# A mixture of experts on one core: the second product of five experts by seven block products, and the searches for their tokens in two queues

## The chip, the cores and the metric

The kernel runs on one core of one Trainium2 chip. The metric is the device time of one execution in microseconds (us). Before the change it is 1454.23 us, the median of 3 runs (1453.94 to 1454.76). The engines are called as in the profile: PE (TensorE: matmuls, and PEld for its weight loads), DVE (VectorE), ACT (ScalarE), POOL (GpSimd, which also issues the indirect DMAs) and SP (SyncE, which issues DMAs).

## What is computed

Four sublayers follow each other on 4 x 1024 tokens of 256 numbers, each with a layer norm and a residual. The first three are an attention in groups, a low-rank feed-forward and a 16-head attention with relu weights; the change does not touch them. The fourth is a mixture of 8 experts in which each expert chooses its own 1024 of the 4096 tokens:

```python
def _L1_ffn_ref(x, Wg, W1, b1, W2, b2):
    n = b * l                                   # 4096 tokens
    k = min(max(int(n * C / e), 1), n)          # 1024 for each of 8 experts
    xt = x.reshape(n, h)                        # h = 256
    S = jax.nn.sigmoid(xt @ Wg).T
    G, I = jax.lax.top_k(S, k)
    ex = xt[I]
    hid = jax.nn.gelu(jnp.einsum('ekh,ehf->ekf', ex, W1) + b1[:, None, :], approximate=False)
    out = (jnp.einsum('ekf,efh->ekh', hid, W2) + b2[:, None, :]) * G[..., None]   # 1024 -> 256
    new_x = jnp.zeros_like(xt).at[I.reshape(-1)].add(out.reshape(-1, h))
```

All matmuls spoken of here are in f32.

## The kernel before

The expert part begins at about 960 us of the span. Tokens are held in 32 tiles of 128 (NTILE), an expert's 1024 chosen tokens in 8 chunks of 128 (NC = 8). An expert is worked in two halves of 512 tokens (TB = 512, NJ = 4 chunks each); `u = 2 * e + q` counts the halves through all experts.

**Search and list.** The top 1024 scores of an expert are found by a search for the threshold, bit by bit. `Search` does it for several experts at once: `compare` (lines 1819 to 1831) compares the scores with seven tried values, one VectorE instruction (L1824) per expert, and counts (L1831); a `tick` (L1833) adds the counts up over the partitions by one small matmul (L1838), keeps the best value on VectorE and compares again. `List` turns a threshold into indices: `sort`, `rank`, `chunks`, `places` (VectorE, L1971), `collect` (matmuls, L1981) and `gather`, which makes the indices and starts eight indirect DMAs on GpSimd (L2005) that fetch the token rows `got`. The search and list of expert 0 stand ahead of the expert part. All others are steps of one list, `agenda`: Search(1), the list of 1, Search(2, 3), the lists of 2 and 3, Search(4, 5, 6, 7), the lists of 4 to 7. Each step carries an estimate of its VectorE time and the first half `u` in which it may be done (`behind`). `go_on_with_lists(u, time)` (L2357) is called at many places of the matmul loops with the time that has passed there, and hands out the next step when the last one is reckoned to be done. Three pieces of Search(1), a compare and two ticks, are written ahead of the first half (loop at L2380).

**First product.** `turn` (L2168) transposes the gathered rows by TensorE (L2176) and copies them to `xT` (L2182). In `feed_forward` (L2276) a half has eight steps `f`, each with two matmuls of 512 columns (L2291) and a gelu on ScalarE into `hid` (L2298). Experts 3 to 6 take both halves together in `feed_forward_by_seven` (L2226): the 2 x 2 block product (blocks over the 256 inputs, the 1024 hidden numbers and the two halves) is made with seven block products of sums and differences instead of eight. It has four steps `f`, each with seven matmuls (L2237), five additions on VectorE (L2252 to L2266) and four gelus. The sums of weight blocks that it needs are made by four GpSimd instructions (`weight_sums`, L2201), the sums of token blocks by four VectorE instructions (`token_sums`, L2208).

**Second product.** `project_back` (L2308) goes over the four chunks of a half: eight matmuls of 256 columns into one PSUM tile (L2317), `y = (py + bias) * gate` in two VectorE instructions (L2332, L2333), and an indirect DMA on GpSimd that adds the rows `y` to their tokens in DRAM (L2334). An expert's scatters wait for the ones of the expert before. There are seven `y` tiles. The transposes of the next half stand between the chunks (`turns_within`, L2210). Expert 7 adds to `accg` instead (L2328), and works on the closing layer norm beside its matmuls (`aside`).

The order on each engine is that in which the program writes the instructions, save where the tile scheduler moves one; for GpSimd it is the written order from expert 6 on (`manual_schedule`). Rooms that the change uses again: `accg` and `xg`, two 128 x 8 x 256 tiles that expert 7 needs at the end, and `wq1`, `wk1`, `wv`, weights of the third sublayer.

Of the kernel before, what the change touches and what calls it, by code (L numbers as in the profile page):

```python
# [9 lines left out]
F32 = mybir.dt.float32  # L10
# [3 lines left out]
AF = mybir.ActivationFunctionType  # L14
ALU = mybir.AluOpType
# [4 lines left out]
P = 128  # L20
D = 256
DC = D // P
TB = 512
# [51 lines left out]
def kernel(  # L75
# [1679 lines left out]
    with ExitStack() as st4:  # L1755
# [135 lines left out]
        class List:  # L1891
# [58 lines left out]

            def steps(self):

                behind = max(QPE * self.e - 3, 0)
                return [
                    (0.5, behind, self.sort),
                    (2.6, behind, self.rank),
                    (1.2, behind, self.chunks),
                    (1.4, behind, lambda: (self.places(0), self.places(1))),
                    (1.4, behind, lambda: (self.places(2), self.places(3))),
                    (0.3, behind, lambda: [self.collect(part) for part in range(4)]),  # L1960

                    (0.3, behind + 1, self.gather),
                ]

            def places(self, part):
# [199 lines left out]
        QPE = NC // NJ  # L2165
        xT = {}

        def turn(u, c, half=None):  # L2168

            if c == 0 and not half:  # L2170
                xT[u] = wk.tile([P, DC, TB], F32, tag="xT", name="xT")
            e, q = divmod(u, QPE)
            tiles = range(NJ) if half is None else range(half * NJ // 2, (half + 1) * NJ // 2)
            tp = ps.tile([P, NJ, P], F32, tag="mm", name="tp", bufs=5)
            for i in tiles:
                nc.tensor.transpose(tp[:, i, :], lists[e].got[q * NJ + i][:, c * P : (c + 1) * P], ident)  # L2176
                if u == 0 and c == 0 and i == 0:

                    keep_busy(first, 4)
            cols = slice(tiles[0] * P, (tiles[-1] + 1) * P)  # L2180
            copy = nc.scalar.copy if by_seven(e) else nc.vector.tensor_copy
            copy(xT[u][:, c, cols], tp.rearrange("p j t -> p (j t)")[:, cols])  # L2182

        def by_seven(e):

            return 3 <= e < NE - 1

        rooms = [x.rearrange("p j d -> p (j d)")[:, h * TB : (h + 1) * TB] for x in xs[:4] for h in range(2)]
        seven = dict(zip(("sum0", "T1", "sum1", "T2", "T4", "S1", "S2", "S4"), rooms))
# [13 lines left out]
        def token_sums(e, n):  # L2203

            (b11, b21), (b12, b22) = ([xT[QPE * e + q][:, c, :] for c in range(DC)] for q in range(QPE))
            t1, t2, t4 = (seven[name] for name in ("T1", "T2", "T4"))
            dst, x, y = ((t1, b12, b11), (t2, b22, t1), (b12, b22, b12), (t4, b21, t2))[n]
            nc.vector.tensor_tensor(dst, x, y, ALU.subtract)  # L2208

        def turns_within(u):  # L2210

            e, q = divmod(u, QPE)
            if u == QPE * NE - 1:
                return {}
            turns = {c: (lambda c=c: turn(u + 1, c)) for c in range(DC)}
            if q == QPE - 1 and by_seven(e + 1):
                both = [
                    turns[0], turns[1], lambda: turn(u + 2, 0), lambda: token_sums(e + 1, 0), lambda: turn(u + 2, 1),
                    *(lambda n=n: token_sums(e + 1, n) for n in (1, 2, 3)),
                ]  # L2220
                return {0: both[0:1], 1: both[1:4], 2: both[4:]}
            if by_seven(e) and q == 0:
                return {}
            return {2: [turns[0], turns[1]]} if u == 1 else {1: [turns[0]], 2: [turns[1]]}

        def feed_forward_by_seven(e):  # L2226

            w1, w2 = weights[e]
            hid = [wk.tile([P, FC, TB], F32, tag="hid", name="hid") for _ in range(QPE)]
            (b11, b21), (t3, b22) = ([xT[QPE * e + q][:, c, :] for c in range(DC)] for q in range(QPE))  # L2230
            t1, t2, t4 = (seven[name] for name in ("T1", "T2", "T4"))
            half = DFF // 2
            s3 = w1[:, 0, half:DFF]
            s1, s2, s4 = (seven[name] for name in ("S1", "S2", "S4"))

            def product(bank, a, b, start, stop, f):
                nc.tensor.matmul(bank, lhsT=a[:, f * P : (f + 1) * P], rhs=b, start=start, stop=stop, skip_group_check=not start)  # L2237

            gelus = []

            def gelu(n, f, src):
                gelus.append(nc.scalar.activation(hid[n][:, f, :], src, AF.Gelu, bias=mb1[:, e * FC + f : e * FC + f + 1]))

            HC = FC // 2
            for f in range(HC):
                a, b, c, d = (ps.tile([P, TB], F32, tag="mm", name=f"ph{k}", bufs=5) for k in range(4))
                u2 = seven[f"sum{f % 2}"]
                c22, c21, c12 = hid[1][:, HC + f, :], hid[0][:, HC + f, :], hid[1][:, f, :]
                product(a, w1[:, 0, 0:half], b11, True, True, f)
                nc.scalar.copy(u2, a)  # L2250
                product(b, s2, t2, True, True, f)
                nc.vector.tensor_tensor(u2, u2, b, ALU.add)  # L2252
                product(c, s3, t3, True, True, f)
                nc.vector.tensor_tensor(c22, u2, c, ALU.add)
                product(d, s1, t1, True, True, f)
                nc.vector.tensor_tensor(c22, c22, d, ALU.add)
                product(a, w1[:, 1, 0:half], b21, False, True, f)
                gelu(0, f, a)
                if f < HC - 1:
                    go_on_with_lists(QPE * e, 3.2, True)  # L2260
                gelu(1, HC + f, c22)
                product(c, w1[:, 1, half:DFF], t4, False, True, f)
                nc.vector.tensor_tensor(c21, u2, c, ALU.add)
                gelu(0, HC + f, c21)
                product(d, s4, b22, False, True, f)
                nc.vector.tensor_tensor(c12, u2, d, ALU.add)  # L2266
                gelu(1, f, c12)
                go_on_with_lists(QPE * e, 3.0)
            for q in range(QPE):
                if q == 0 and by_seven(e + 1):  # L2270
                    weight_sums(e + 1, gelus[-1])
                if q == 0 and e == NE - 2:
                    fetch_last()
                project_back(QPE * e + q, hid[q])

        def feed_forward(u):  # L2276
            e, q = divmod(u, QPE)
            w1, w2 = weights[e]
            hid = wk.tile([P, FC, TB], F32, tag="hid", name="hid")

            n = TB if u else TB // 2
            for h in range(TB // n):
# [3 lines left out]
                for f in range(FC):  # L2286
# [13 lines left out]
                    )  # L2300
                    if u or h or f not in (FC - 5, FC - 4, FC - 3):
                        go_on_with_lists(u, 1.75 if u else 0.87)
                    aside(u, "f", f)
            if q == QPE - 1 and by_seven(e + 1):
                weight_sums(e + 1, gelu)
            project_back(u, hid)

        def project_back(u, hid):  # L2308

# [2 lines left out]
            ahead = turns_within(u)  # L2312
            for i in range(NJ):
                k = q * NJ + i
                py = ps.tile([P, D], F32, tag="y", name="py")
                for f in range(FC):
                    nc.tensor.matmul(  # L2317
                        py,
                        lhsT=hid[:, f, i * P : (i + 1) * P],
                        rhs=w2[:, f, :],  # L2320
                        start=(f == 0),
                        stop=(f == FC - 1),
                    )
                for do in ahead.get(i, ()):
                    do()
                gates = lists[e].got[k][:, D + e : D + e + 1]
                if e == NE - 1:
                    nc.vector.scalar_tensor_tensor(accg[:, k, :], py, gates, accg[:, k, :], ALU.mult, ALU.add)  # L2328
                    aside(u, "i", i)
                    continue  # L2330
                y = wk.tile([P, D], F32, tag="y", name="y", bufs=7)
                nc.vector.tensor_tensor(y, py, mb2[:, e, :], ALU.add)  # L2332
                nc.vector.tensor_scalar(y, y, gates, None, ALU.mult)  # L2333
                scatter = nc.gpsimd.indirect_dma_start(  # L2334
# [7 lines left out]
                )  # L2342
                after_all(scatter, scattered[e - 1] if e else ())
                beside_each_other(scatter, scattered[e])
                go_on_with_lists(u, 3.4 if by_seven(e) else 2.3)

        searches = [Search(0), Search(1), Search(2, 3), Search(4, 5, 6, 7)]
        agenda = []  # L2350
        for search in searches[1:]:
            agenda.extend(search.steps())
            for e in search.es:
                agenda.extend(lists[e].steps())
        left = [0.0]

        def go_on_with_lists(u, time, within=False):  # L2357
            left[0] = max(left[0] - time, 0.0)
            if agenda and left[0] < 0.3 and agenda[0][1] <= u and not (within and agenda[0][0] not in (0.5, 1.2, 1.4)):
                spent, _, step = agenda.pop(0)  # L2360
                left[0] += spent
                step()

        first = ps.tile([P, TB], F32, tag="mm", name="idle", bufs=5)
        def first_places():
# [12 lines left out]
            if step == lists[0].rank:  # L2378
                keep_busy(first, 8)
        for _ in range(3):  # L2380
            agenda.pop(0)[2]()
            keep_busy(first, 4)
        def fetch_last():

# [49 lines left out]
```

## Time and profile before

| | |
|---|---|
| median of 3 runs | 1454.23 us |
| profiled execution: its time, its span | 1461.5 us, 1459.7 us |
| mean granted TensorE clock of it | 0.983 |
| busy in the span: PE, DVE, ACT, POOL | 1407.1, 863.5, 735.9, 531.2 us |
| second product, L2317: 1024 records of matmuls | 230.6 us busy, mean 382 ns |
| first product, L2291: 288 records | 114.8 us busy |
| scatters, L2334: 56 | 88.1 us busy on POOL |
| window 1050 to 1110 us: PE, DVE, ACT, POOL busy | 60.00, 29.35, 11.26, 21.20 us |
| window 1110 to 1170 us | 59.64, 41.52, 13.50, 25.41 us |
| window 1333 to 1388 us, granted clock 0.97 | 51.87, 24.34, 13.15, 27.27 us |
| window 1388 to 1460 us, granted clock 0.95 | 61.90, 39.56, 26.90, 40.78 us |

A row of the groups view reads: line, engine, operation, output <- inputs, shape, count, then busy time in us, mean duration of one in ns, then the idle time before the instructions with what ended it. Matmuls overlap in the array, so the mean duration of one is longer than the distance from one to the next; the distance is read from the timeline, where a row gives start, length and the number of records in it. An f32 matmul leaves two records.

### The profile page before, as it was taken

Reading aid. Unit: us, or ns where it says so; the run is one execution under the profiler, and the core shown is the slowest. Engines: PE = TensorE matmul, PEld = TensorE weight load, DVE = VectorE, ACT = ScalarE, POOL = GpSimd, SP = SyncE. Lnnn points to the kernel's source line nnn. Section 1 sums busy time; section 2 is a strip of 40 time slices with the busy share of each in tenths; the row PEclk is TensorE's granted clock in tenths of the full one; section 3 lists DMA queues with packets and bytes.
Section 4 is the critical chain, followed back from the end, with each engine's and each line's share of the span. In section 5 each row is a group of like instructions: output and inputs, shape, how many; then the busy total and the mean of one; then the engine's idle time right before and its main releaser. Section 6 shows DMA issues by size and latency. Waiting matters only on the chain.

```text
span 1459.7 us, 26465 instructions
## 1 busy us (share of the span) xinstructions
PE 1407.1 (96%) x10392; PEld 859.7 (59%) x10392; DVE 863.5 (59%) x2133; ACT 735.9 (50%) x1014; POOL 531.2 (36%) x662
## 2 busy tenths in 40 slices
PE   8999999999889999999999999949999999999997
PEld 4666666666644445454454547717666656756674
DVE  5457555666454637664757486885545766355246
ACT  4244454444368887878778788712221232232143
POOL 4123322322352223423333223413425325543655
PEclk9999999999999999999999999979999999999998
DMA  8400000001652373537244711152414223333365
GB/s 223 140 1 1 0 1 1 1 1 40 206 166 83 115 223 94 154 117 233 73 142 149 227 59 35 46 163 41 106 26 121 50 84 69 78 97 58 76 168 133
DMA packets 104853, 138.76 MB, mean 95 GB/s; under 512 B 25469, under 2 KB 64794, under 8 KB 104602
## 3 DMA queue, kind: packets, MB, share of 16 engines
q1 hardware_dynamic: 74512, 81.75, 18.2%
q0 software_dynamic: 30160, 55.32, 16.3%
q8 instruction: 81, 1.33, 0.4%
q14 instruction: 42, 0.34, 0.1%
q10 hardware_dynamic: 58, 0.01, 0.0%
HBM read 75.29 MB, written 61.51 MB: 94 GB/s over the span
## 4 chain that ended last, share of the span: by engine, by line
PE 86%; DVE 6%; issue 2%; DMA 2%; POOL 2%; ACT 1%; another core or an unknown queue 1%; SPq 0%; POOLq 0%; DVEq 0%; ACTq 0%
PE po L1553 16%; PE py L2317 14%; PE sc L1532 10%; PE ph L2237 7%; PE ph L2291 7%; PE pg L722 4%; PE pv L738 4%; PE py L848 3%; PE pt L1308 2%; PE pq L397 2%; PE po L820 2%; PE ph L904 2%; PE pv L431 2%; PE po L824 1%; PE pkv L835 1%
## 5 line engine op out<-in xcount | busy, mean ns | idle before, releaser
L1710 ACT ACTIVATE w<-sc 128x1024 f32<-128x1024 f32 x395 | 379.9, 1023 | 60.8 <-PE sc L1532 60.2
L1553 PE MATMUL po<-w,vaug 128*17 128x256 f32 (+1 forms) x4608 | 256.0, 358 | 1.5 <-DVE turned L1611 1.2
L2317 PE MATMUL py<-w,hid 128*128 128x256 f32 x1024 | 230.6, 382 | 3.1 <-DVE y L2332 3.1
L2317 PEld LDWEIGHTS py<-w,hid 128*128 128x128 f32 x1024 | 193.1, 191 | 33.5 <-issue 4.4
L1712 DVE TENSOR_SCALAR w<-sc 128x1024 f32<-128x1024 f32 x117 | 142.4, 1220 | 79.5 <-PE sc L1532 76.1
L1553 PEld LDWEIGHTS po<-w,vaug 128*17 128x17 f32 x4608 | 116.3, 97 | 118.0 <-issue 48.3
L1532 PE MATMUL sc<-q,kT 64*128 64x512 f32 (+1 forms) x1152 | 170.3, 404 | 2.5 <-ACT w L1710 1.3
L1532 PEld LDWEIGHTS sc<-q,kT 64*128 64x128 f32 x1152 | 89.9, 185 | 83.5 <-issue 46.7
L2334 POOL DMA_INDIRECT acc_d<-y,idx x56 | 88.1, 1574 | 119.8 <-DVE y L2333 59.5
L2298 ACT ACTIVATE hid<-ph,mb 128x512 f32<-128x512 f32 (+1 forms) x72 | 46.1, 640 | 164.8 <-PE ph L2291 137.2
L2291 PE MATMUL ph<-xT,w 128*128 128x512 f32 (+1 forms) x288 | 114.8, 552 | 0.3 <-DVE xT L2182 0.3
L2005 POOL DMA_INDIRECT got<-tok_d,idx x64 | 66.9, 1045 | 113.0 <-DVE idx L1995 96.0
L2291 PEld LDWEIGHTS ph<-xT,w 128*128 128x128 f32 x288 | 52.6, 190 | 51.3 <-issue 48.5
L371 POOL DMA_DIRECT2D kT<-k_d x32 | 23.4, 732 | 118.4 <-PE sc L1532 55.4
L2332 DVE TENSOR_TENSOR y<-py,mb 128x256 f32<-128x256 f32 x56 | 23.5, 420 | 71.8 <-PE py L2317 51.7
L722 PE MATMUL pg<-nT,wh 128*128 128x512 f32 x128 | 61.6, 613 | 1.5 <-ACT nT L661 1.5
L848 PE MATMUL py<-wo,oT 128*128 128x256 f32 x256 | 61.6, 384 | 0.0
L738 PE MATMUL pv<-wh,nT 128*128 128x512 f32 x128 | 59.7, 592 | 0.0
L848 PEld LDWEIGHTS py<-wo,oT 128*128 128x128 f32 x256 | 47.5, 190 | 17.6 <-issue 11.1
L746 ACT ACTIVATE v<-v 128x512 f32<-128x512 f32 x32 | 20.2, 630 | 62.7 <-DVE v L745 62.7
L1137 POOL TENSOR_TENSOR rsb<-veb,mhalf 128x1 f32<-128x1 f32 x30 | 19.6, 653 | 86.8 <-DVE veb L1136 86.8
L586 POOL TENSOR_TENSOR x<-x,y 128x1024 f32<-128x1024 f32 x13 | 30.6, 2355 | 56.3 <-ACT y L575 56.3
(352 smaller groups left out, 2338.0 us busy)
## 6 DMA issues: line engine op xcount, KB each, us to landing
q<-q_d POOLq DMA_DIRECT2D x16, 1024.0 KB
kT<-k_d POOLq DMA_DIRECT2D x32, 512.0 KB
w<-in_L_ffn_W_dram SPq DMA_DIRECT2D x16, 1024.0 KB
k_d<-parts SPq DMA_DIRECT2D x48, 256.0 KB
q_d<-parts SPq DMA_DIRECT2D x48, 256.0 KB
acc_d<-logits SPq DMA_DIRECT2D x8, 512.0 KB
tok_d<-hg SPq DMA_DIRECT2D x30, 128.0 KB
x<-in_L_attn_x_dram SPq DMA_DIRECT2D x7, 512.0 KB
```

The lines of the kernel that those rows point to most:

```text
L722: nc.tensor.matmul(pg, lhsT=wh[:, c, HID + e * P : HID + (e + 1) * P], rhs=d["nT"][:, c, :], start=(c == 0), stop=(c == DC - 1),)
L738: nc.tensor.matmul(pv, lhsT=d["nT"][:, c, i * P : (i + 1) * P], rhs=wh[:, c, 0:HID], start=(c == 0), stop=(c == DC - 1),)
L848: nc.tensor.matmul(py, lhsT=d["oT"][:, e, :], rhs=wo[:, e, :], start=(e == 0), stop=(e == EC - 1))
L1532: nc.tensor.matmul(sc[:, j, m * n : (m + 1) * n], lhsT=row["kT"][t, r][rows, u, (kt + m) * P : (kt + m + 1) * P], rhs=row["q"][qh, t][rows ...
L1553: nc.tensor.matmul(po[rows : rows + HD + 1, at : at + n], lhsT=row["v"][:, kt + m, HQ * t + 4 * r + 2 * u + j, :], rhs=w[:, j, (2 * m + pa ...
L1710: nc.scalar.activation(w, sc, AF.Relu)
L1712: nc.vector.tensor_scalar(w, sc, 0.0, None, ALU.max)
L2005: return nc.gpsimd.indirect_dma_start(out=dst, out_offset=None, in_=rows[:, :], in_offset=self.at_chunk(c), bounds_check=NT - 1, oob_is_er ...
L2237: nc.tensor.matmul(bank, lhsT=a[:, f * P : (f + 1) * P], rhs=b, start=start, stop=stop, skip_group_check=not start)
L2291: nc.tensor.matmul(ph, lhsT=w1[:, c, f * P : (f + 1) * P], rhs=xT[u][:, c, h * n : (h + 1) * n], start=(c == 0), stop=(c == DC - 1),)
L2317: nc.tensor.matmul(py, lhsT=hid[:, f, i * P : (i + 1) * P], rhs=w2[:, f, :], start=(f == 0), stop=(f == FC - 1),)
L2334: scatter = nc.gpsimd.indirect_dma_start(out=acc_d[:, :], out_offset=lists[e].at_chunk(k), in_=y, in_offset=None, bounds_check=NT - 1, oob ...
```

## The change

Experts 1 to 5 make their second product like this, for both halves together (new function `project_back_by_seven`; `by_seven`, that is the first product, stays with experts 3 to 6): the blocks are the two halves of tokens (`hid[0]`, `hid[1]`), the two halves of the 1024 hidden numbers, and the two halves of the 256 outputs.

```diff
+            sub, plus = ALU.subtract, ALU.add
+            p1 = new_bank("p1")
+            product(p1, a11, b11, True, True)
+            nc.scalar.copy(u2, p1)
+            nc.vector.tensor_tensor(s1, a21, a22, plus)
+            nc.vector.tensor_tensor(s3, a11, a21, sub)
...
+            p4 = new_bank("p4")
+            product(p4, a22, t4, True, True)
+            nc.vector.tensor_tensor(s2, s1, a11, sub)
...
+            product(p1, a12, b21, False, True)
+            of_bias(0)
+            for k in range(NJ):
+                add(k, 0, p1)
+            summed_up = nc.vector.tensor_tensor(s4, a12, s2, sub)
+            if by_seven(e + 1):
+                weight_sums(e + 1, summed_up)
...
+            p5 = new_bank("p5")
+            product(p5, s1, t1, True, True)
+            nc.scalar.copy(kept, p5)
...
+            p6 = new_bank("p6")
+            product(p6, s2, t2, True, True)
+            nc.vector.tensor_tensor(u2, u2, p6, plus)
+            of_bias(1)
...
+            p7 = new_bank("p7")
+            product(p7, s3, t3, True, True)
+            nc.vector.tensor_tensor(v, u2, p7, plus)
+            nc.vector.tensor_tensor(c21, v, p4, plus)
+            nc.vector.tensor_tensor(v, v, kept, plus)
+            for k in range(NJ, NC):
+                put_off.append(lambda k=k: add(k, 0, c21))
+                put_off.append(lambda k=k: (add(k, 1, v), put(k)))
...
+            product(p5, s4, b22, False, True)
+            nc.vector.tensor_tensor(u2, u2, p5, plus)
+            put_off.extend(lambda k=k: (add(k, 1, u2), put(k)) for k in range(NJ))
```

A `product` is 16 matmuls of 128 columns into one PSUM tile of 128 x 512. `of_bias` starts four `y` tiles with bias times gate on ScalarE; `add` adds gate times one 128 x 128 block to half of a `y` tile on VectorE; `put` scatters a `y` tile. The four sums s1 to s4 are of 128 x 2048 and go to `accg` and over blocks of `hid`; the output sums go to `xg`.

```diff
+            def product(bank, a, b, start, stop):
+                for i in range(NJ):
...
+                    for f in range(HC):
+                        nc.tensor.matmul(
+                            bank[:, i * P : (i + 1) * P],
+                            lhsT=a[:, f, i * P : (i + 1) * P],
+                            rhs=b[:, f, :],
...
+            def of_bias(q):
+                for k in range(q * NJ, (q + 1) * NJ):
+                    ys[k] = wk.tile([P, D], F32, tag="y", name="y", bufs=9)
+                    nc.scalar.activation(ys[k], mb2[:, e, :], AF.Identity, scale=gates[k])
+
+            def add(k, n, src):
...
+                nc.vector.scalar_tensor_tensor(y, src[:, i * P : (i + 1) * P], gates[k], y, ALU.mult, ALU.add)
```

The weight block sums t1 to t4 are made on GpSimd in the first f step of the same expert (experts 3 to 5) or of its second half (experts 1 and 2):

```diff
+        def back_sums(e, behind):
+
+            (b11, b12), (b21, b22) = back_blocks(e)
+            t1, t2, t4 = (room.rearrange("p (f n) -> p f n", n=P) for room in back_rooms)
+            for dst, x, y in ((t1, b12, b11), (t2, b22, t1), (b12, b22, b12), (t4, b21, t2)):
+                after_all(nc.gpsimd.tensor_tensor(dst, x, y, ALU.subtract), [behind])
```

The twelve pieces `put_off` of an expert (twelve additions, eight scatters) are done in the f loop of the next expert, six behind each of the first two steps of a loop by seven, three behind each step of an ordinary one:

```diff
                 gelu(1, f, c12)
-                go_on_with_lists(QPE * e, 3.0)
+                if f == 0 and back_by_seven(e):
+                    back_sums(e, gelus[-1])
+                if put_off:
+                    for _ in range(min(6, len(put_off))):
+                        put_off.pop(0)()
+                if not put_off:
+                    go_on_with_lists(QPE * e, 3.0)
...
+                    for _ in range(min(3, len(put_off))):
+                        put_off.pop(0)()
+                    if back_by_seven(e) and not q and f in (FC - 5, FC - 2):
+                        turn(u + 1, int(f == FC - 2), tag="y")
+                    if back_by_seven(e) and q and not f:
+                        back_sums(e, gelu)
```

So the weight sums for the next expert's first product start behind s4 and no longer behind the last gelu, the transposes beside the new product use PSUM tiles of the tag "y", the copies of experts 1 and 2 to `xT` go from VectorE to ScalarE, and there are nine `y` tiles.

The searches are cut differently, and the two parts have a queue each; the second is served where the first has nothing that may be done:

```diff
-        searches = [Search(0), Search(1), Search(2, 3), Search(4, 5, 6, 7)]
-        agenda = []
+        searches = [Search(0), Search(1, 2, 3), Search(4, 5, 6, 7)]
+        agendas = []
...
+            for agenda in agendas:
+                if agenda and agenda[0][1] <= u:
+                    if within and agenda[0][0] not in (0.5, 1.2, 1.4):
+                        return
+                    spent, _, step = agenda.pop(0)
+                    left[0] += spent
+                    step()
+                    return
...
-            agenda.pop(0)[2]()
+            agendas[0].pop(0)[2]()
```

A list may be made from half `2e - 4` on instead of `2e - 3`; its gather stays at `2e - 2`. Inside expert 0's second product `go_on_with_lists` is called twice per chunk with 1.5 us instead of once with 2.3.

## The prediction

> **What bounds the kernel now.** I read the page's busy times and chain first, then what TensorE waited for in the expert part (1000 to 1460 us of the span).
>
> ```profile
> PE 1407.1 (96%) x10392; PEld 859.7 (59%) x10392; DVE 863.5 (59%) x2133; ACT 735.9 (50%) x1014; POOL 531.2 (36%) x662
> ...
> PE 86%; DVE 6%; issue 2%; DMA 2%; POOL 2%; ACT 1%; another core or an unknown queue 1%; SPq 0%; POOLq 0%; DVEq 0%; ACTq 0%
> ```
> ```profile
> PE py L2317 <- DVE y L2332: 3.1, 1, 3.1
> PE parts L1838 <- DVE counts L1831: 0.4, 1, 0.4
> ```
>
> TensorE sets the end: from 1000 to 1460 us only these two waits of it are listed. So TensorE time saved there counts in full, and so does every new wait of TensorE. The other engines come next, in windows of two whole experts, e = 3 and e = 4 (columns: length, then busy time of PE, PEld, DVE, ACT, POOL):
>
> ```profile
> 1170.00:1224.50 54.50, 54.50 (x237) 37.20 (x236) 33.38 (x73) 15.26 (x25) 25.55 (x20) 1.00 0.35 78
> 1224.50:1279.00 54.50, 54.50 (x235) 36.79 (x234) 26.92 (x60) 15.39 (x25) 25.79 (x20) 1.00 0.35 78
> ```
>
> VectorE has 21 to 28 us to spare per expert, and the clock is 1.00 there. Now the TensorE timeline, for the second product as it is and for a stream of matmuls with 128 columns and their own f32 weights, earlier in the program:
>
> ```profile
> 1194.95 17.51 PE L2317 MATMUL py<-w,hid 128*128 128x256 f32 x80
> 1212.30 0.60 PE L2176 MATMUL tp<-ident,got 128*128 128x128 f32 x4
> ```
> ```profile
> 311.99 0.38 PE L820 MATMUL po<-packed,v 128*128 128x128 f32 x2
> 312.21 0.39 PE L824 MATMUL po<-head,kv 128*128 128x128 f32 x2
> ...
> 313.77 1.06 PE L688 MATMUL psim<-head,head 128*128 128x128 f32 x8
> 314.66 1.88 PE L722 MATMUL pg<-nT,wh 128*128 128x512 f32 x4
> ```
>
> One f32 matmul leaves two records. 80 records of 256 columns take 1212.30 - 1194.95 = 17.35 us, 0.2169 each. From 311.99 to 314.66 stand 24 records of 128 columns: 2.67 us, 0.1113 each, a little over half.
>
> **The product.** An expert's second product is 8 tiles x 8 = 64 matmuls: 128 records x 0.2169 = 27.76 us. The seven products have 7 x 4 x 4 = 112 matmuls of 128 columns: 224 x 0.1113 = 24.93. Gain 2.83 per expert, 14.15 for five. Lower bound of the new cadence is half the old, 0.1084 (another 0.65 per expert). The upper bound is the weight load:
>
> ```profile
> L2317 PEld LDWEIGHTS py<-w,hid 128*128 128x128 f32 x1024 | 193.1, 191 | 33.5 <-issue 4.4 <-DVE y L2332 3.5 <-DVE accg L2102 0.2
> ...
> L820 PEld LDWEIGHTS po<-packed,v 128*128 128x128 f32 x256 | 39.2, 192 | 7.2 <-issue 5.3 <-DVE sta L558 1.0 <-DVE sth L558 0.2
> ```
>
> Could loads not overlap, 224 x 0.19 = 42.6 us would be 14.8 more than now, per expert. The L820 stream has a load of 192 ns for every record and still goes on every 111 ns, so I take 0.1113. (The Trainium skill, "TensorE: Matmul & The Clock Gate", section "Back-to-back issue gap", speaks against the change: a stream in which each matmul has its own weight load runs at about 81 ns at 128 columns and not the 56 ns of a lone matmul; estimated from that page, 25 ns on each of 224 records would be 5.6 us per expert, and the whole about 24 us above the sum below. The stream of line 820, f32, shows no such surcharge.)
>
> Searching experts 1 to 3 at once takes ten ticks (line 1838) off TensorE. Before, a tick's 0.17 us overlaps its neighbours and moves the matmuls on by some 0.07: 0.7 us, and perhaps the one 0.4 wait. Gains: 14.15 + 0.7 + 0.4 = 15.2 us.
>
> **What the other engines get.** Rows for VectorE (column after the bar: busy total, mean ns of one):
>
> ```profile
> L2333 DVE TENSOR_SCALAR y<-y,got 128x256 f32<-128x256 f32 x56 | 24.4, 435 | 2.0
> L2332 DVE TENSOR_TENSOR y<-py,mb 128x256 f32<-128x256 f32 x56 | 23.5, 420 | 71.8 <-PE py L2317 51.7 <-PE parts L1838 9.7 <-remote 7.6
> ...
> L2208 DVE TENSOR_TENSOR x<-xT,x 128x512 f32<-128x512 f32 x8 | 5.5, 688 | 4.4 <-ACT xT L2182 4.4
> ```
>
> Out go 8 x (0.42 + 0.435) = 6.8 us. In come four sums of 128x2048, at most four times 0.688 each: 11.0; five additions of 128x512 on PSUM: 3.4; sixteen scaled additions of 128x128, between half of and all of the 0.48 of line 2328's 128x256, say 0.35: 5.6. That is +13 us: some 46 of e = 3's 51.7 us. It fits, with 5 left. ScalarE gets ten passes of about 0.59 (its 128x512 copy, line 2182): 15.3 + 5.9. GpSimd gets four sums of 128x512 at 1.28 to 1.47 (line 2201): 25.7 + 5.4, and issue gaps of 0.3 behind each of 16 indirect DMAs. The scatters are as many as before; twelve put-off pieces stand in the next expert's f loop, four scatters with each result half. Nine y tiles for seven let them end later; the next expert's scatters come some 30 us after. In GpSimd's queue the next list's gathers, 8 x 1.3 = 10.5 us, fall behind them; the lists may begin half an expert earlier, the gathers in the same half as before, and the transposes need the rows some 25 us later. SyncE's queue is passed by nothing. None of these three engines is filled; all of it costs nothing, unless a piece is late for TensorE. These are the places.
>
> **Start.** Three pieces of the second search stand on VectorE ahead of the first xT copy:
>
> ```profile
> 988.75 0.76 DVE L2182 COPY xT<-tp 128x256 f32<-128x256 f32 x2 [1.07 <-PE idle L203]
> ```
>
> Now a compare and reduce are 0.39 + 0.39, a piece repeats every 1.67 us, and they end at 987.68. For three experts, between the two-expert 0.62 and four-expert 1.09 reduces, a pass is about 0.98 + 0.86 = 1.84, a piece 2.7: 983.52 + 1.84 + 2 x 2.7 = 990.8. The copy is 2.1 us later, and nothing else runs on TensorE. Loss 2.1 (1.5 to 2.5).
>
> **VectorE against GpSimd.** The trace shows what happens where a GpSimd sum meets a VectorE operation with two SBUF inputs; VectorE and then GpSimd:
>
> ```profile
> 1151.09 1.30 DVE L1824 TENSOR_TENSOR ge<-by_e,tried 128x224 bf16<-128x224 f32 x4
> ...
> 1154.63 4.52 DVE L1824 TENSOR_TENSOR ge<-by_e,tried 128x224 bf16<-128x224 f32 x4
> ```
> ```profile
> 1154.70 1.45 POOL L2201 TENSOR_TENSOR x<-w 128x512 f32<-128x512 f32 x1 [12.81 <-ACT hid L2298]
> 1156.23 1.30 POOL L2201 TENSOR_TENSOR w<-w 128x512 f32<-128x512 f32 x1
> 1157.49 1.41 POOL L2201 TENSOR_TENSOR x<-x,w 128x512 f32<-128x512 f32 x1
> 1158.98 1.30 POOL L2201 TENSOR_TENSOR x<-w,x 128x512 f32<-128x512 f32 x1
> ```
>
> The four compares take 4.52 us for 1.30: held 3.2 us. VectorE operations that read PSUM (line 2332, 0.42 at 1209.05 beside such a sum) are not. The change puts four more sums on GpSimd per expert, and on VectorE sums and put-off additions with two SBUF inputs, so it makes more such meetings. (The Trainium skill, "GPSIMD Engine Reference", section "1. Specifications", says the two share their SBUF interfaces, with contention for VectorE instructions with two SBUF inputs or in a two-port mode; the trace agrees with the 3.2 us above, and that page gives no price.) Each place costs between 0 and one full hold of 3.2 us:
>
> - Expert 1's second half: its four back sums start with the first gelu, 2.7 us in, for 5.4 us, beside the first compares for experts 4 to 7. A four-expert tick is 3.5 us on VectorE (1151.09 to 1154.63), TensorE comes to the next one after two f steps, 3.45 us: no cover. Half of the 3.2 hold: 1.4.
> - Expert 2's first half: twelve put-off additions (12 x 0.3 = 3.6 us) beside the same ticks, three per f step. No slack, but only four f steps: 0.9 (0 to 3.6).
> - Experts 3 to 5, f = 2: an f step is 14 records in 6.0 us. GpSimd goes scatter, first sum, scatter, three sums, which I place at 11.5 to 15.5 us; the second six put-off additions start at 12.9, held to 15.5, done at about 16.6; then line 2252's and 2254's 1.3 us: 17.9. TensorE's sixth product needs them at 12.0 + 5 x 0.86 = 16.3. Loss 1.6 each, 4.8.
> - Experts 3 to 5, between the last products: next expert's weight sums now start behind s4, some 40 us in, beside list places and token sums on VectorE, whose collecting matmuls (line 1981) stand on TensorE. Some cover, so 0.6 each, 1.8.
>
> Behind each held VectorE operation waits TensorE's next product into the same bank, and nothing else.
>
> **Sum.** Gains 15.2; losses 2.1 + 1.4 + 0.9 + 4.8 + 1.8 = 11.0; net 4.2 us. Against the profiled execution's own time, 1461.5 (span 1459.7), that is 1457.3. It stands 7.3 above the median of the runs, 1454.23; the difference carries over: 1450.0.
>
> **Rivals.**
> - All meetings hide: additions slip between two sums, as one 0.37 us line 2333 at 1309.26 did. Only the start stays: 15.2 - 2.1 = 13.1, 1441. Against it: 1154.63. Chance 0.17.
> - The meetings eat the gain: 2.5 us more lost than I take, spread over e = 3 to 5, 1452 to 1456. Chance 0.18.
> - Slower: the shared access makes VectorE the bound of experts 3 to 5. Price: 3.2 at f = 2 and 3.2 at the weight sums, 6.4 x 3 = 19.2, with 4.4 elsewhere: 23.6 - 15.2 = +8, 1462. It decides from 3.7 us lost per expert on ((15.2 - 4.4) / 3 = 3.6). For it: +13 us of VectorE work with 5 us left; against: most of that work is early. Chance 0.15.
> - Weight loads bound: 5 x 14.8 = 74 for -14, so some 1539, or a part of it. Against: line 820. Chance 0.10 for any form that loses.
> - The 3.1 us wait behind line 2332 at 1373 (expert 6, untouched) goes away with the shifted order: 1447. I count it within my case. That the change does not do what it says is out: in the changed order of instructions TensorE has the 112 short matmuls.
>
> **How the numbers follow.** My case has 0.40, 1446 to 1453. A measurement of this kernel tells 0.2%, 2.9 us, from no change. Faster: 0.36 of my case and 0.17: 0.53. Same: 0.04 and 0.15: 0.19. Slower: 0.03 + 0.15 + 0.10: 0.28. The range takes the first two rivals and most of the third's way up: 1440 to 1461; the bounds of all losses (1.5 to 28) would give 1440 to 1467.
>
> **What would show it.** The new product's timeline at 0.111 us per record, 24.9 us per expert; the first L2291-type matmul 2.1 us later; TensorE idle before the sixth product of f = 2 in experts 3 to 5, with VectorE additions of 128x128 or compares stretched to over 1 us beside GpSimd sums. Wrong if records come at over 0.124 (the whole gain), or if TensorE waits for scatters, y tiles or banks, which I cost at nothing.

## The result, and the profile after

The changed kernel is slower: 1479.68 us, median of 4 runs (1478.34 to 1482.05), beside 1454.09 for the kernel before (median of 4); ratio 1.0179 (95% interval 1.0161 to 1.0196). On another chip the ratio was 1.0134 (1.0112 to 1.0157). The profiled execution took 1478.96 us, its span is 1477.2 us, the clock 0.977. From its page, busy times, chain and three groups:

```profile
PE 1402.5 (95%) x10862; PEld 867.8 (59%) x10862; DVE 930.0 (63%) x2131; ACT 762.2 (52%) x1072; POOL 579.6 (39%) x681
...
PE 81%; DVE 8%; DMA 3%; issue 3%; POOL 3%; ACT 1%; SPq 0%; POOLq 0%; DVEq 0%; ACTq 0%
...
L2354 POOL DMA_INDIRECT acc_d<-y,idx x40 | 64.2, 1606 | 72.3 <-ACT x L2256 62.5
...
L2334 PEld LDWEIGHTS p<-w,hid 128*128 128x128 f32 x640 | 73.0, 192 | 2.9 <-issue 2.9
L2334 PE MATMUL p<-w,hid 128*128 128x128 f32 x640 | 74.3, 276 | 0.0
```

TensorE is busy for less (1402.5 for 1407.1) and the span is 17.5 longer: the work got shorter, the waits longer. What TensorE waited for from 960 us on (total, times, longest):

```profile
PE parts L1838 <- DVE counts L1831: 16.7, 12, 1.8
PE ph L2243 <- DVE hid L2260: 9.4, 3, 3.2
PE p L2334 <- POOL wv L2305: 7.4, 1, 7.4
PE py L2464 <- ACT hid L2438: 3.9, 2, 3.1
```

Before there were 3.1 and 0.4 us in the part from 1000 us on. Of the first row 2.0 us are from there; the rest are ticks ahead of expert 0's first matmul. The product itself does what was asked of it; TensorE's timeline in expert 3:

```profile
1207.28 3.73 PE L2334 MATMUL p<-w,hid 128*128 128x128 f32 x32
1210.85 3.74 PE L2334 MATMUL p<-wv,hid 128*128 128x128 f32 x32
1214.42 3.74 PE L2334 MATMUL p<-w,hid 128*128 128x128 f32 x32
```

32 records start every 3.57 us: 0.1116 us each. I then cut the expert part into stages, from the first matmul of one expert to that of the next in the TensorE timeline (us; "start" is from the indices of expert 0, L1995, to its first xT copy; the tail is expert 7 to the end of the span). Two executions of each kernel:

| | start | e0 | e1 | e2 | e3 | e4 | e5 | e6 | tail |
|---|---|---|---|---|---|---|---|---|---|
| before | 5.6 | 60.5 | 60.3 | 59.6 | 55.0 | 55.0 | 55.1 | 59.1 | 65.9 |
| before, second | 5.6 | 60.5 | 60.2 | 59.6 | 55.0 | 55.0 | 55.1 | 57.7 | 66.0 |
| changed | 8.8 | 61.3 | 58.1 | 68.1 | 57.5 | 58.7 | 57.5 | 52.7 | 72.9 |
| changed, second | 9.2 | 63.2 | 58.1 | 66.9 | 58.5 | 57.7 | 58.6 | 59.8 | 66.5 |

Against the second execution of before the stages add up to 20.8 and 23.7 us more: expert 2 has 7 to 9 of it, experts 3 to 5 have 9 to 10, the start 3 to 4. Experts 6 and 7 must be taken together (125.0 and 123.7 before, 125.5 and 126.2 after).

**Expert 2.** GpSimd's timeline in the changed kernel, and then TensorE's:

```profile
1113.40 1.04 POOL L2005 DMA_INDIRECT got<-tok_d,idx  x1 [39.03 <-DVE y L2351]
...
1139.46 1.57 POOL L2354 DMA_INDIRECT acc_d<-y,idx  x1 [0.30 <-issue]
1140.48 1.85 POOL L2305 TENSOR_TENSOR wq<-w 128x512 f32<-128x512 f32 x1
1142.41 3.21 POOL L2305 TENSOR_TENSOR wk<-w,wq 128x512 f32<-128x512 f32 x1
1145.57 3.31 POOL L2305 TENSOR_TENSOR w<-w 128x512 f32<-128x512 f32 x1
1148.85 1.71 POOL L2305 TENSOR_TENSOR wv<-w,wk 128x512 f32<-128x512 f32 x1
```
```profile
1150.61 6.71 PE L2334 MATMUL p<-wv,hid 128*128 128x128 f32 x32 [7.39 <-POOL wv L2305]
```

VectorE is at its first sum, s1, meanwhile:

```profile
1140.40 4.09 DVE L2370 TENSOR_TENSOR accg<-hid 128x2048 f32<-128x2048 f32 x1 [1.49 <-ACT hid L2438]
```

Eight gathers of the next list and eight put-off scatters keep GpSimd from 1113 to 1141; only then do the four back sums start, and the second product waits 7.4 us for the last of them. The sums themselves take 10.1 us from the first to the end of the last, beside s1 and s3 on VectorE; with VectorE out of the way four of them take 5.1 (in the run "Nothing put off" below). The 32 records behind the wait then take 6.5 us (to 1157.15) instead of 3.6, at a mean granted clock of 0.54; in the second profile they take 5.0.

**Experts 3 to 5, step f = 2.** The put-off additions in the steps f = 0 and f = 1, six each, on VectorE in expert 3; GpSimd meanwhile; TensorE:

```profile
1184.81 1.66 DVE L2351 SCALAR_TENSOR_TENSOR y<-xg,got,y 128x128 f32<-128x128 f32 x6
...
1190.82 5.30 DVE L2351 SCALAR_TENSOR_TENSOR y<-xg,got,y 128x128 f32<-128x128 f32 x6
```
```profile
1190.40 1.82 POOL L2305 TENSOR_TENSOR wk<-w,wq 128x512 f32<-128x512 f32 x1
1191.64 1.80 POOL L2305 TENSOR_TENSOR w<-w 128x512 f32<-128x512 f32 x1
1192.86 1.79 POOL L2305 TENSOR_TENSOR wv<-w,wk 128x512 f32<-128x512 f32 x1
```
```profile
1197.64 2.07 PE L2243 MATMUL ph<-x,w 128*128 128x512 f32 x2 [3.06 <-DVE hid L2260]
1199.51 1.78 PE L2243 MATMUL ph<-xT,x 128*128 128x512 f32 x2
```

The second six take 3.64 us longer, and end 1.5 us after the last of the three sums. And the matmuls behind the wait are slow. The windows of this stretch, with the granted clock in the column before the last two:

```profile
1194.50:1197.60 3.10, 0.08 (x1) 0.00 (x0) 2.98 (x9) 0.69 (x1) 2.63 (x3) 1.00 0.20 18
1197.60:1202.20 4.60, 4.56 (x9) 1.92 (x10) 2.55 (x8) 1.59 (x3) 3.83 (x3) 0.63 0.64 74
1202.20:1208.00 5.80, 5.80 (x20) 2.92 (x19) 4.68 (x14) 3.00 (x5) 4.74 (x4) 1.00 0.69 77
```

Over 4.6 us the mean granted clock is 0.63. The three products after the wait start 1.87, 1.67 and 0.95 us apart instead of 0.86: another 1.9 us. This wait costs 5 us, not 3. It isn't always so. In the second profile of the changed kernel the same wait has matmuls at full speed behind it:

```profile
1197.45 1.12 PE L2243 MATMUL ph<-x,w 128*128 128x512 f32 x2 [3.06 <-DVE hid L2260]
```

The two profiles of the changed kernel and three of the variants below have fifteen waits of 3.06 to 3.24 us at this place. Behind ten of them the granted clock falls: three of three in the first profile, one of three in the second.

### The profile page after: what moved, and what is told of

Same layout as the page of the kernel before. It is cut to its first block, busy times and chain, and to the rows that moved or that the text cites. A ratio compares the mean times of both kernels' runs of the same rounds, so it can differ in the third digit from the quotient of the medians.

```text
span 1477.2 us, 27534 instructions
## 1 busy us (share of the span) xinstructions
PE 1402.5 (95%) x10862; PEld 867.8 (59%) x10862; DVE 930.0 (63%) x2131; ACT 762.2 (52%) x1072; POOL 579.6 (39%) x681
## 4 chain that ended last, share of the span: by engine, by line
PE 81%; DVE 8%; DMA 3%; issue 3%; POOL 3%; ACT 1%; SPq 0%; POOLq 0%; DVEq 0%; ACTq 0%
PE po L1553 15%; PE sc L1532 10%; PE p L2334 8%; PE ph L2243 6%; PE ph L2431 5%; PE pg L722 4%; PE py L2464 4%; PE pv L738 4%; PE py L848 4%; PE pq L397 2%; PE pt L1308 2%; PE po L820 2%; PE ph L904 2%; PE pv L431 2%; PE pk L397 2%
## 5 line engine op out<-in xcount | busy, mean ns | idle before, releaser
L2005 POOL DMA_INDIRECT got<-tok_d,idx x64 | 76.9, 1201 | 96.1 <-DVE y L2351 39.0
L2438 ACT ACTIVATE hid<-ph,mb 128x512 f32<-128x512 f32 (+1 forms) x72 | 46.0, 638 | 125.7 <-PE ph L2431 95.3
L2354 POOL DMA_INDIRECT acc_d<-y,idx x40 | 64.2, 1606 | 72.3 <-ACT x L2256 62.5
L2464 PE MATMUL py<-w,hid 128*128 128x256 f32 x384 | 87.9, 386 | 3.9 <-ACT hid L2438 3.9
L2431 PEld LDWEIGHTS ph<-xT,w 128*128 128x128 f32 x288 | 52.7, 190 | 51.5 <-issue 48.6
L2464 PEld LDWEIGHTS py<-w,hid 128*128 128x128 f32 x384 | 72.8, 193 | 16.6 <-ACT hid L2438 4.7
L2334 PEld LDWEIGHTS p<-w,hid 128*128 128x128 f32 x640 | 73.0, 192 | 2.9 <-issue 2.9
L2334 PE MATMUL p<-w,hid 128*128 128x128 f32 x640 | 74.3, 276 | 0.0
L848 PE MATMUL py<-wo,oT 128*128 128x256 f32 x256 | 61.6, 384 | 0.0
L586 POOL TENSOR_TENSOR x<-x,y 128x1024 f32<-128x1024 f32 x13 | 30.6, 2355 | 56.3 <-ACT y L575 56.3
```

Source lines behind the costliest of these rows:

```text
L848: nc.tensor.matmul(py, lhsT=d["oT"][:, e, :], rhs=wo[:, e, :], start=(e == 0), stop=(e == EC - 1))
L2005: return nc.gpsimd.indirect_dma_start(out=dst, out_offset=None, in_=rows[:, :], in_offset=self.at_chunk(c), bounds_check=NT - 1, oob_is_er ...
L2334: nc.tensor.matmul(bank[:, i * P : (i + 1) * P], lhsT=a[:, f, i * P : (i + 1) * P], rhs=b[:, f, :], start=start and not i and not f, stop= ...
L2431: nc.tensor.matmul(ph, lhsT=w1[:, c, f * P : (f + 1) * P], rhs=xT[u][:, c, h * n : (h + 1) * n], start=(c == 0), stop=(c == DC - 1),)
L2464: nc.tensor.matmul(py, lhsT=hid[:, f, i * P : (i + 1) * P], rhs=w2[:, f, :], start=(f == 0), stop=(f == FC - 1),)
```

## The experiments

All ratios are to the kernel before on the same chip. The second profile of the kernel before and the first three variants are from one chip (kernel before: 1460.58 us); no run of the changed kernel stands beside them. The other variants are from another one (1459.40 and 1459.51 us), on which the changed kernel stands at 1.0134 (1.0112 to 1.0157):

> The changed kernel timed beside the kernel before on the chip of this group. The ratio was 1.0179 on the first chip, while the two profiled executions differ by 1.2% only, and the variants that undo one cost each stand at 1.007 to 1.013 on other chips. If the changed kernel has one price everywhere, 1.016 to 1.020 again; if the first chip's runs of the kernel before were fast for a reason of their own (no wait in expert 6), 1.011 to 1.015.

The price is 19 us there (1478.83 for 1459.51). The kernel before is what differs between the chips, 1454.1 and 1459.5; the changed kernel hardly does. The ratio is that of the second case, but no profile shows that its reason, a wait missing in expert 6, is the right one. A second profile of the kernel before asked what its own first one (1461.5) held:

> The kernel before, profiled a second time. Its first profiled execution (1461.5 us) lies 7.3 above the median of its runs; there TensorE waits 3.1 us in expert 6 and the expert takes 59.1 us, the three experts ahead of it 55.0 to 55.1. If that wait belongs to one execution only, this profile shows expert 6 at about 55 us without a wait of over 1 us and the time near 1454, and then the change costs some 25 us and not the 17.5 that the two profiles differ by. If the wait belongs to the program, it is there again, at some 1461.

It took 1458.21 us, and the wait in expert 6 was there again, 3.4 us. So it isn't an accident of one execution; whether the runs of 1454 us on the first chip had it, no profile shows.

**The searches as before.** One queue, Search(1) and Search(2, 3), lists from 2e - 3 on, the old times (and 1.7 instead of 0.35 per call within the new product, so that the lists are ready).

```diff
-        searches = [Search(0), Search(1, 2, 3), Search(4, 5, 6, 7)]
+        searches = [Search(0), Search(1), Search(2, 3), Search(4, 5, 6, 7)]
```

> The changed kernel with the searches as before: Search(1), Search(2, 3), Search(4, 5, 6, 7) in one queue, the lists from half 2e - 3 on. Theory: the three longer pieces ahead of the first xT copy cost 3.2 us between the indices of expert 0 and that copy (8.8 us against 5.6), which comes back; expert 2, where the wait for the back sums stands, stays slow or gets slower, as the ticks for experts 4 to 7 move into it. Time 1475 to 1483. Rival, that the merged search is what costs most: under 1465.

1492.28 us, ratio 1.0215 (1.0200 to 1.0229): worse than the changed kernel, and above the range I gave it. The start is 5.6 us again; expert 2 takes 70.1 us, as the ticks for experts 4 to 7 now wait there, beside the back sums (4.35, 2.17 and 1.36 us before L1838), experts 3 to 6 57 to 64. So the new queues alone are not what makes the change slow.

**Expert 2's back sums ahead of the 16 indirect DMAs.**

```diff
+                    if e == 2 and not q and not f:
+                        back_sums(e, gelu)
...
-                    if back_by_seven(e) and q and not f:
+                    if e == 1 and q and not f:
```

> The changed kernel with the back sums of expert 2 issued behind the first gelu of its first half, ahead of the 16 indirect DMAs on GpSimd's queue, and not behind the first gelu of its second half. Theory: the 7.4 us wait of TensorE's second product for the last back sum, and the 3.0 us that the same 16 matmuls ran longer behind it, are the price of the place in GpSimd's queue; both go, at a new cost of 0 to 4 us beside the ticks and the put-off additions in the first half: 1469 to 1474. Rival, that VectorE's sums s1 and s2 are what is late there: the wait stays, on a VectorE line, and the time stays within 3 us of 1479.7.

1474.70 us, 1.0098 (1.0084 to 1.0113). The wait for L2305 is gone, and expert 2 takes 62.7 us for 66.9 to 68.1. It isn't the 57 that the product promises, for the sums now meet the compares of a tick; VectorE's timeline:

```profile
1115.52 5.40 DVE L1824 TENSOR_TENSOR ge<-by_e,tried 128x224 bf16<-128x224 f32 x4
```

1.30 undisturbed, and the tick's matmul waits 3.8 us. The place in the queue was the cause of the one wait, and the new place has the other.

**Nothing put off.** Additions and scatters at once, in the place where they were appended to the list.

```diff
-                put_off.append(lambda k=k: add(k, 0, c21))
-                put_off.append(lambda k=k: (add(k, 1, v), put(k)))
+                add(k, 0, c21)
+                add(k, 1, v)
+                put(k)
...
-            put_off.extend(lambda k=k: (add(k, 1, u2), put(k)) for k in range(NJ))
+            for k in range(NJ):
+                add(k, 1, u2)
+                put(k)
```

> The changed kernel without putting off: the twelve additions and eight scatters of experts 1 to 5 are done as soon as their blocks are there. Theory, GpSimd's place and its hold on VectorE: the f = 2 waits of experts 3 to 5 go (3 x (3.1 + 1.9 slow clock) = 15 us), expert 2's back sums start earlier (up to 10), and expert 6's queue on GpSimd is done some 8 us earlier, so that the tail after it shrinks by 4 to 7: 1448 to 1456. Rival, that VectorE is simply full: the same additions wait at another place, and the time stays above 1470.

1470.13 us, 1.0068 (1.0054 to 1.0082). Expert 2 is at 57.1 us, experts 6 and 7 together at 122.3, as expected. Expert 2's sums are still behind 16 indirect DMAs, eight scatters and then eight gathers, but GpSimd's queue now begins at the start of the expert: the sums run from 25.8 to 30.9 us into it (1136.22 to 1141.30 us; 30.6 to 40.7 in the changed kernel), done before VectorE comes to s1 at 1143.45, which then takes 2.29 us and not 4.09, and TensorE does not wait for them. But experts 3 to 5 stay at 58.1, 59.4 and 58.7. The sums come later now and meet other work; VectorE in expert 3:

```profile
1188.07 4.69 DVE L1971 TENSOR_TENSOR at<-lo,each 128x1024 bf16<-128x1024 bf16 x2
```

1.29 us undisturbed. Half of the expectation fell. The time is where the rival put it, above 1470, but its reason, the same additions waiting at another place, is not what the rows show: what is left in common is not the put-off additions but the sums beside whatever VectorE does with two SBUF inputs.

**The sums moved, the put-off pieces left.** The back sums of experts 3 to 5 start behind the last addition of the product before (`added`).

```diff
+            if back_by_seven(e):
+                back_sums(e, added[-1])
...
-                if f == 0 and back_by_seven(e):
-                    back_sums(e, gelus[-1])
...
-            nc.vector.tensor_tensor(u2, u2, p5, plus)
+            added.append(nc.vector.tensor_tensor(u2, u2, p5, plus))
```

> The changed kernel with the back sums of experts 3 to 5 issued at the start of the expert, behind the last addition of the product before, where VectorE has only operations with one operand in PSUM, and no longer behind the first f step. Theory, GpSimd's sums hold VectorE's operations with two SBUF inputs: the six put-off additions take 1.7 us in f = 2 as in f = 1 and not 5.3, TensorE's 3.1 us waits there go and the slow clock behind them (1.9 each): 15 us less than the changed kernel, ratio to the kernel before 1.006 to 1.010. Rival, the put-off additions are too many in VectorE's order whatever GpSimd does: the waits stay and the ratio is above 1.014.

1468.82 us, 1.0069 (1.0053 to 1.0084). The waits at f = 2 are gone: experts 3 to 5 take 54.2, 54.0 and 54.2 us for 57.5 to 58.7. GpSimd's sums and the same six additions of f = 1 in expert 3, on VectorE:

```profile
1179.60 1.27 POOL L2305 TENSOR_TENSOR wq<-w 128x512 f32<-128x512 f32 x1 [9.05 <-DVE xg L2410]
...
1183.40 1.28 POOL L2305 TENSOR_TENSOR wv<-w,wk 128x512 f32<-128x512 f32 x1
```
```profile
1191.46 1.66 DVE L2351 SCALAR_TENSOR_TENSOR y<-xg,got,y 128x128 f32<-128x128 f32 x6
```

The same number of instructions in the same place of VectorE's order, 1.66 us instead of 5.30 with the sums out of the way. That settles this term. The sums themselves take 1.27 and not 1.8. The whole is 10 us below the changed kernel, not 15: expert 6 and the tail take 127.8 us here, and TensorE waits 4.0 us in experts 3 to 5 for rows of the next list.

**Two search pieces at the start** (`range(3)` to `range(2)` in the loop ahead of expert 0).

> The changed kernel with two pieces of the merged search ahead of the first xT copy and not three. Theory: from the indices of expert 0 to that copy it takes 8.8 us, 5.6 before; one tick fewer takes 2.8 of VectorE's time and its TensorE gap of 1.8 us away, so 5.6 to 6.2, and the time is 2 to 3 us below the changed kernel's: ratio 1.0155 to 1.0175. Rival, that the tick comes back as a wait in expert 0 or as a later list: same time as the changed kernel.

1477.34 us, 1.0128 (1.0112 to 1.0145), the same as the changed kernel within what can be told. The start is 5.8 us, as expected; but expert 0 takes 64.9 us. List 1 comes later, and TensorE waits for its rows before the transposes (two waits of 1.0 us, and a granted clock of 0.73 and 0.81 in the windows there). The rival was right. How the third piece makes 3.2 us out of 2.1 can be read from TensorE's timeline of the changed kernel:

```profile
986.36 0.18 PE L1838 MATMUL parts<-counts,all_b 128*128 128x24 bf16 x1 [1.78 <-DVE counts L1831]
986.39 1.87 PE L203 MATMUL idle<-all_b 128*128 128x512 bf16 x4
...
988.26 1.59 PE L203 MATMUL idle<-all_b 128*128 128x512 bf16 x4
989.69 0.49 PE L2176 MATMUL tp<-ident,got 128*128 128x128 f32 x3
```

The four filler matmuls that keep TensorE busy took 1.02 us before and take 1.87 and 1.59 here, behind idle times of 1.55 and 1.78, and the transposes stand behind them; VectorE had been done at 989.1. The mean granted clock is 0.67 from 985 to 988 us and 0.77 from 988 to 991; in the kernel before it is 1.00 in both. That the clock is the reason I read from these rows; no run tested it alone.

**The last expert's own rows.** `fetch_last` (eight gathers, 10.5 us) moved from expert 6 to steps f = 3 and f = 6 of expert 7's second half.

> The changed kernel with the eight gathers of the last expert's own rows (xg, 10.5 us on GpSimd) taken out of expert 6's queue and done in expert 7's second half. In the changed kernel GpSimd works from 1360 to 1411 us without a break and the last scatter of expert 6 is issued 7.0 us after expert 7 has begun (2.8 before), and the tail, expert 7 to the end, takes 72.9 us (65.9 before). Theory, GpSimd's queue is what is late: expert 6 at some 52.6 us and the tail back at 65 to 67, 5 to 7 us off: ratio 1.013 to 1.0145. Rival, the tail is bound by read-backs whatever the queue: the tail stays at over 71 us.

1474.51 us, 1.0118 (1.0100 to 1.0135). Expert 6 and tail take 52.7 + 69.0 = 121.7 us, 4 less than in the changed kernel; the tail falls, but not to 67. The interval overlaps that of the changed kernel, so the time alone doesn't show a gain. In the changed kernel GpSimd's queue runs without a pause through expert 6:

```profile
1359.89 1.77 POOL L2354 DMA_INDIRECT acc_d<-y,idx  x1 [14.70 <-ACT x L2256]
...
1409.75 1.54 POOL L2483 DMA_INDIRECT acc_d<-y,idx  x1 [0.30 <-issue]
1414.44 1.08 POOL L2005 DMA_INDIRECT accg<-acc_d,idx  x1 [3.15 <-DMA acc_d<-y,idx]
```

**Put together, first try:** nothing put off, sums first, two pieces.

> Nothing put off, back sums of experts 3 to 5 at the start of the expert, two search pieces at the start. Theory: the run without putting off stood at 1.0068 with f = 2 waits of 3.6 to 3.8 us and slow clock behind them in three experts, 18 us with what follows; with these gone and 2 to 3 us at the start the ratio is 0.992 to 0.996, the seven products' gain at last. Rival, the holds move on to list places or to s1 to s4, or scatters behind the sums hold up the next list's gathers: above 1.0.

1459.60 us, 1.0006 (0.9996 to 1.0016): no change. Without put-off pieces the eight scatters of expert 2 are written ahead of expert 3's sums, and three of the four sums run behind them, in the list work; VectorE there:

```profile
1181.53 4.96 DVE L1931 SCALAR_TENSOR_TENSOR place<-place,chosen 128x32 f32<-128x32 f32 x1
```

An instruction of 0.19 us is held for 4.8, TensorE waits 4.35, expert 3 takes 59.4 us; expert 0 takes 64.7.

**Second try ("best2" in the next expectation):** sums first for experts 3 to 5, pieces put off for experts 2 to 4 only, `fetch_last` late, searches as in the change.

```diff
+            while e in (1, 5) and put_off:
+                put_off.pop(0)()
```

> Back sums of experts 3 to 5 at the start of the expert; pieces put off for experts 2 to 4 alone, at once for experts 1 and 5; the last expert's own rows gathered in its second half. Sum of the stages as the earlier runs had them: experts 1 and 2 at 58 and 57 us, 3 to 5 at 54.2, 6 at 52.7, the tail at 66 to 69, start and expert 0 as in the changed kernel (4 us more than before): 5 to 9 us less than the kernel before, ratio 0.993 to 0.997. Rival, the scheduler's order on GpSimd moves the holds elsewhere: 1.0 or more.

1454.92 us, 0.9970 (0.9959 to 0.9980): faster than both kernels, 4.6 us less than before, at the upper end of the expectation. All that TensorE waited for from 990 us on:

```profile
PE tp L2180 <- DMA got<-tok_d,idx: 4.3, 3, 1.5
PE parts L1838 <- DVE counts L1831: 1.7, 1, 1.7
PE parts L1981 <- DVE y L2488: 1.4, 1, 1.4
PE parts L1981 <- issue: 0.2, 1, 0.2
```

The stages: expert 0 63.3, then 58.1, 57.1, 54.4, 54.0, 54.2, 52.7 and 68.9 us. With Search(1) and Search(2, 3) in the first queue again (and 0.7 for 0.35 per call within the new product):

> As best2, and the first queue of searches as before, Search(1) and then Search(2, 3), with Search(4 to 7) in the second queue. Theory: the 3.2 us at the start come back, ten more ticks cost 0.7 us, and the ticks for experts 4 to 7 fall into expert 2, beside its back sums, where each hold is 1 to 4 us: ratio 0.990 to 1.002, and the profile shows which is larger. Rival, that the start is worth nothing as expert 0's first tokens are late anyway: not below best2.

1466.57 us, 1.0055 (1.0034 to 1.0075). The start is at 5.6 us, expert 0 at 61.6, but expert 2 at 62.3 (a tick's matmul waits 3.6 us), experts 3 to 5 at 56 to 58, with waits of 2.1 for the next list's rows at each turn: what is saved in front is lost behind. It lies above the range I gave it.

## Why the prediction was wrong

- *The product, 2.83 us per expert:* right. 0.1116 per record instead of 0.1113; no load of weights shows as a wait, and the 25 ns more per record did not come. (Five times 5.6 us would have been 28 above the sum and 24 above the kernel before; the prediction says 24 above the sum.) Where nothing is late, experts 3 to 5 are at 54.0 to 54.4 with some 1.4 us of waits for rows within (55.0 before).
- *"None of these three engines is filled; all of it costs nothing, unless a piece is late for TensorE. These are the places":* this step failed. Expert 2's second half, the dearest place, is not among the places. I counted GpSimd's work by share of an expert, and looked for what is queued behind the DMAs only in the gathers. The back sums of expert 2 stand behind 16 indirect DMAs in the same queue: 7.4 us, and 3.0 for the slow matmuls after (7.7 and 1.5 in the second profile). I had 0.9 for expert 2's first half, from another mechanism, which took 0.3. The run with the sums ahead of the DMAs shows that the place in the queue is the cause; it is without this wait. The place is not the whole price, though. The first product is done 33.1 us into the expert. Sums that start at 30.6 and take 5.1, as in the run with nothing put off, would end at 35.7: my estimate is a wait of 2.5 us by the queue alone. The other 5 us come from the meeting with s1 and s3, into which the late start pushes the sums, and for which the prediction has no term.
- *Experts 3 to 5 at f = 2, 1.6 us each:* the place and the mechanism were right, shown by the run with the sums moved; the size was off by three. The last three sums ran 12.4 to 16.7 us into the expert (I had 11.5 to 15.5). I let the held additions be done 1.1 us after the sums; they ended 1.5 after the last sum, so TensorE waited 3.1. And I had no term for the clock behind the wait, 1.9 where it falls. The three cost 15 us in the first profile and some 11 in the second (9.4 of waits, one fall of the clock), not 4.8.
- *The start, 2.1:* 3.2 to 3.6. VectorE's share was right (its pieces end 7.9 us after the indices, 4.6 before; I had 3.1 more); the fillers ahead of the transposes were not in the sum. Taking one piece away moved the loss to expert 0.
- *Expert 1's second half, 1.4:* 1.7, right. *Weight sums, 0.6 each, 1.8 in all:* too much. TensorE waits once at L1981, 1.1 us in expert 4, and in the second profile not at all.
- *Expert 6 and the tail:* costed at nothing; 0.5 to 2.5 us against before. The eight put-off scatters fill GpSimd's queue in expert 6. *Expert 0* had no term either: 0.8 and 2.7 us longer, and no run shows why. *Rows of the next list*, of which I said that they are needed some 25 us later: no wait in the first profile, 4.5 us in experts 3 and 5 in the second.
- *The sum:* -4.2 forecast, 20.8 and 23.7 by the stages. Expert 2 (some 10) and f = 2 (6 to 10) make most of the difference.
- *The rivals:* the slower one named the right access and its price per hold, 3.2, and stayed at +8 because it left the clock and GpSimd's order out. That all meetings hide, or only eat the gain, is out by the waits above. The loads of weights are out by the 0.1116.

Open: what the y addition in expert 6 waits for (3.1 and 3.4 us in the two profiles of before, none in one of the two of the changed kernel, 4.4 in the other); why the profile without it has 3.9 us of waits for gelus (L2438) in expert 7 instead, as if expert 6 and tail traded against each other; and why the kernel before ran 5 us faster on the first chip. None was tried.

## What to carry to other kernels

Before work is given to an engine that is half idle, write down its queue in order and mark what another engine needs from it: in this kernel the wait was made by what stood ahead, not by the share of busy time. Put sums on GpSimd where VectorE works from PSUM; beside VectorE work with two SBUF inputs they cost up to a full hold here. And price a wait of three microseconds on TensorE at three to five, for behind most of them, not all, the clock fell.

## What was not expected of the hardware

- A held VectorE instruction can end only with the last of a row of GpSimd sums, however short it is: 4.96 us for one of 128x32 that takes 0.19. It isn't so everywhere. In the kernel before, the four compares at 1154.63 ended 1.1 us before the last of the four sums did; in expert 2 of the run with nothing put off, three short instructions (L1931, L1933, L1935) were held for one sum each, 1.30, 1.18 and 1.20 us. What makes the difference no run tested.
- GpSimd can pay as well: in expert 2 sums of 1.27 us took 3.2 to 3.3 beside VectorE sums of 128x2048, of which L2370 took 4.09 instead of 2.28. The 1.8 us of the sums in step f = 1 are not such a price. The one at 1187.38 took 1.83 while VectorE's additions from PSUM there took their usual 0.69; and beside the held compares of the run with expert 2's sums moved ahead, the sums took 1.26 to 1.28.
- After 3.1 us without a matmul the mean granted clock was 0.63 over the next 4.6 us, but behind ten of fifteen such waits only. Behind idle times of 1.55 and 1.78 us at the start four fillers took 1.87 us instead of 1.02.
